# Linear layers as two 64-column matmuls side by side, the last step's two pairs transposed by TensorE, and the experts' pieces laid out anew in an attention and expert kernel

## The chip, the cores and the metric

The kernel runs on one core of a Trainium2 chip, in one launch. The metric is the device time in microseconds (us) of that core; lower is better. Times of a kernel are the median of several runs. The profile, with a trace behind it, belongs to one further execution.

## The reference, cut to what matters

For each of 8 batches of 512 tokens with 256 features, the input is normalised; then attention with 16 heads of 64 features (rotary positions on q and k, a bias that falls with the distance) and a layer of 16 experts, of which each token takes one, both read the normalised input, and the sum of input and both is the output.

```python
qkv = (x @ qkv_w.T).reshape(Bb, Ss, 3, H, D)
...
scores = jnp.einsum('bhqd,bhkd->bhqk', q, k) * SCALE
...
kb = -p * jnp.log1p(a * dist)
attn = jax.nn.softmax(scores + kb[None], axis=-1)
out = jnp.einsum('bhqk,bhkd->bhqd', attn, v)
...
return out @ out_w.T
...
h = jax.nn.relu(jnp.einsum('ecm,emf->ecf', dispatched, w1))
expert_out = jnp.einsum('ecf,efm->ecm', h, w2)
gathered = expert_out[idx, jnp.minimum(loc, C - 1)]
...
x = x + _L0_attn_ref(xn, ...) + _L0_ffn_ref(xn, ...)
```

`x` is 8 x 512 x 256, each expert has w1 of 256 x 1024 and w2 of 1024 x 256 and room for 256 tokens. All is float32.

## The kernel before, in words

**Steps, pairs, units, duos.** The heads go in 4 groups of 4, and a *step* is one group of one batch: 32 steps, s = 0 to 31. A step has two *pairs* of heads (pair 0 and 1), a pair has four blocks of 128 queries (qc 0 to 3). A *unit* is one pair and one block, two units make a *duo*; so a step has four duos (dd = 0 to 3), and the main loop (L850) runs over 128 duos d. The schedule is by hand (L51): each engine's order is that of the program text.

**What a duo does.** In the order of the text: project q or k of a pair of the next step (`project_qk`, L564: two matmuls of 128 x 128 weights and 512 moving columns, and a copy and a rotation on ACT, DVE and POOL); the scores of the two units of the following duo (`score`, L610: for each head a matmul with 64 rows and 512 columns, with bias and minimum on DVE, and the exponential on ACT, which goes to the tile z); in odd duos from the fifth on `attend` (L708: 8 matmuls of 64 columns, one head to each half of the output's partitions) for the pair that was scored a good two duos earlier; `project_out` of step s - 2 in dd 0 (L746); `turn` of the duo's own two units (L640, 32 x 32 transposes in place on DVE); `attended` (L720, normalising the output on DVE); `project_v` in dd 0 and 1 (L587). After a pair's last turn `move` (L646) carries z into pt, transposed by blocks, with 16 DMAs, one for the reciprocals' way through DRAM (rd) and two to bring them back (rb). All of these 19 are issued by SyncE (SP), as are the weights, normalised inputs and the y tiles. `later` (L867) holds DMAs that SP issues in the next duo.

**The experts.** The routing is computed in small parts from duo 16 on (`route`, L311). When it is done the weights of expert 0 are loaded and `begin` is set; from there `expert_work` (L543) yields one *piece* at a time, 8 for each expert: four `expert_hidden` (L507, each 4 products of 256 columns and a relu on ACT) and four `expert_out` (L523, each 4 such products). A duo does 1, 1, 4, and 2 or 3 pieces in dd 0 to 3 (L933). The next expert's input is gathered by POOL after the second piece (`fetch`), transposed by TensorE in the piece with quarter 2 (L554, `expert_in`, L495), and the next weights are put into `later` after the fourth and the eighth piece. The w1 and w2 tiles have two buffers each, one expert's two halves. From duo 108 (`late`, L803) on POOL gathers the experts' output back (`gather`, L759), ACT weighs it and POOL adds it to y.

**PSUM pools.** `ps_sc` has four tiles (scores), `ps_mm` two (q and k, v, output, experts), `ps_av` one, `ps_po` one (experts' output, logits) (L65 to L68).

**The last step.** Pair 1 of step 31 is not turned and moved but goes through `turn_last` (L673): DVE divides z by its sums into zn, TensorE transposes four 128 x 128 blocks of each head into a `ps_mm` tile, and ACT copies them to a tile of its own, which comes from z's three-buffer pool. `attend_last` (L693) is the product with v for it. Pair 0 goes the usual way, by `move`. After the loop (L974 to L983) come attend of (31, 0), attend_last of (31, 1) in two halves and the last output. In duo 127 the text has `attended` of (30, 1) and `project_out` of step 30 ahead of its turn_last (L885 to L886).

Of the kernel before, what the change touches and what calls it, by code (L numbers as in the profile page):

```python
# [33 lines left out]
def attention_and_experts(  # L34
# [472 lines left out]
    def expert_hidden(e, f2):  # L507
        if f2 == 0:
            held["hT", e] = ffn["a"].tile([P, F // P, CAP], F32, tag="hT", name=f"hT_{e}")
        hT, xdT = held["hT", e], held["xdT", e]  # L510
        ph = ps_mm.tile([P, 2, CAP], F32, tag="mm", name=f"ph_{e}_{f2}")
        for i in range(2):
            fc = 2 * f2 + i
            for mc in range(2):
                nc.tensor.matmul(  # L515
                    ph[:, i, :],
                    held["w1", e, fc // 4][:, mc, (fc % 4) * P : (fc % 4 + 1) * P],
                    xdT[:, mc, :],
                    start=(mc == 0), stop=(mc == 1),
                )  # L520
        nc.scalar.activation(hT[:, 2 * f2 : 2 * f2 + 2, :], ph, AF.Relu)

    def expert_out(e, quarter):  # L523
        c, half = divmod(quarter, 2)
        hT = held["hT", e]
        if quarter == 0:
            held["po", e] = ps_po.tile([P, 2, DM], F32, tag="po", name=f"po_{e}")
        po = held["po", e]
        for fc in range(half * 4, half * 4 + 4):
            nc.tensor.matmul(  # L530
                po[:, c, :], hT[:, fc, c * P : (c + 1) * P], held["w2", e, fc // 4][:, fc % 4, :],
                start=(fc == 0), stop=(fc == F // P - 1),
            )
        if quarter == 3:
            ot = ffn["a"].tile([P, 2, DM], F32, tag="eo", name=f"eot_{e}")
            nc.scalar.copy(ot, po)  # L536
            later.append(
                lambda: nc.sync.dma_start(
                    eo[e * CAP : (e + 1) * CAP, :].rearrange("(c p) m -> p c m", p=P), ot
                )  # L540
            )

    def expert_work():  # L543
# [20 lines left out]
    def project_qk(s, pair, part, turn_too=True):  # L564
        g, b = divmod(s, B)
        wq, _ = weights[g]
        ps = ps_mm.tile([P, S], F32, tag="mm", name=f"qk_{s}_{pair}_{part}")
        c0 = part * GC + pair * P
        for mc in range(2):
            nc.tensor.matmul(  # L570
                ps, wq[:, mc, c0 : c0 + P], xnTs[s][:, mc, :], start=(mc == 0), stop=(mc == 1),
            )
# [14 lines left out]
    def project_v(s, i2):  # L587
# [6 lines left out]
        for i in range(2):  # L594
            c0 = (2 * i2 + i) * P
            for mc in range(2):
                nc.tensor.matmul(  # L597
                    ps[:, i, :], xnTs[s][:, mc, c0 : c0 + P], wq[:, mc, 2 * GC :],
                    start=(mc == 0), stop=(mc == 1),
                )  # L600
# [71 lines left out]

    def turn_last(s, pair, qc):  # L673

        if qc == 0:
            pts[s, pair] = zpool.tile([P, 2, TB, S], F32, tag="z", name=f"pt_{s}_{pair}")
        rs = small.tile([P, 2], F32, tag="rs", name=f"rs_{s}_{pair}_{qc}")
        nc.vector.reciprocal(rs, sums[s, pair][:, :, qc])
        for j in range(2):
            zn = rope.tile([P, S], F32, tag="sh", name=f"zn_{s}_{pair}_{qc}_{j}", bufs=3)  # L680
            nc.vector.tensor_scalar(
                zn.rearrange("p (c g k) -> p g c k", g=TB, k=32),
                zts[s, pair][:, j, :, :, qc, :], rs[:, j : j + 1], None, ALU.mult,
            )
            ps = ps_mm.tile([P, TB, P], F32, tag="mm", name=f"zt_{s}_{pair}_{qc}_{j}")
            for kc in range(TB):
                nc.tensor.transpose(ps[:, kc, :], zn[:, kc * P : (kc + 1) * P], ident)
            nc.scalar.copy(pts[s, pair][:, j, :, qc * P : (qc + 1) * P], ps)

    oTs: dict = {}  # L690
    avs: dict = {}

    def attend_last(s, pair, i2):  # L693

        if i2 == 0:
            avs[s, pair] = ps_av.tile([P, S], F32, tag="av", name=f"av_{s}_{pair}")
            oTs[pair] = qkpool.tile([P, S], F32, tag=f"o{pair}", name=f"o_{s}_{pair}", bufs=1)
        av, c = avs[s, pair], slice(i2 * 2 * P, (i2 + 1) * 2 * P)
        for kc in range(TB):
            for j in range(2):  # L700
                c0 = pair * P + j * D
                nc.tensor.matmul(
                    av[j * D : (j + 1) * D, c], vals[s][:, kc, c0 : c0 + D],
                    pts[s, pair][:, j, kc, c], start=(kc == 0), stop=(kc == TB - 1),
                )
        nc.vector.tensor_copy(oTs[pair][:, c], av[:, c])

# [38 lines left out]
    def project_out(s, i2):  # L746
        _, wot = weights[s // B]
        ps = ps_mm.tile([P, 2, DM], F32, tag="mm", name=f"po_{s}_{i2}")
        for i in range(2):
            c0 = (2 * i2 + i) * P  # L750
            for pair in range(2):
                nc.tensor.matmul(  # L752
                    ps[:, i, :], oTs[pair][:, c0 : c0 + P], wot[:, pair, :],
                    start=(pair == 0), stop=(pair == 1),
                )
# [91 lines left out]
    turned_at = {3: 2, 6: 3, 8: 4, 10: 5, 12: 6, 14: 7}  # L847
    routing = route()
    working = begin = None
    for d in range(duos):  # L850
# [8 lines left out]
        if d + 1 < duos:  # L859
            score(*units[2 * d + 2])  # L860
            score(*units[2 * d + 3])
        was = divmod((d - 5) // 2, 2) if half and d >= 5 else None
        if was:
            attend(*was)

# [10 lines left out]
            stores.pop(0)()  # L876


        if dd == 0 and s > 1:
            project_out(s - 2, 0)  # L880
        if d == duos - 1:
            attended(*was)
            project_out(s - 1, 0)
            project_out(s - 1, 1)
            store_y(s - 1, True)  # L885
        (turn_last if final else turn)(*units[2 * d])  # L886
        if was and d < duos - 1:
            attended(*was)
        if d == 1:
            turn_logits(0)  # L890
# [1 line left out]
            turn_logits(1)  # L892
        if d - 1 in turned_at:
            turn_logits(turned_at[d - 1])
        if dd in (0, 1):
# [6 lines left out]
        if dd == 0 and s > 1:  # L902
            project_out(s - 2, 1)
            later.append(lambda s=s: store_y(s - 2, s - 2 >= steps - B + 2))

# [127 lines left out]
```

## Time and profile before

| what | before |
|---|---|
| median of 3 runs | 1273.08 us (1268.95 to 1273.43) |
| the profiled execution's own time | 1280.13 us |
| its span in the trace | 1278.4 us |
| busy: TensorE, DVE, ACT, POOL | 1219.7, 893.5, 611.7, 617.4 us |
| weight loads of TensorE | 670.1 us |
| DMA, SP's queue | 177104 packets, 240.98 MB, 73.6% of 16 engines |
| TensorE's clock, mean of the span | 0.988 of full |

Busy times of different engines overlap. Line numbers such as L570 are lines of the kernel before. In a group's name, `out<-in`, come the tiles by the names of the program: qk, v, sc, av, po and ph are the PSUM tiles of the products. The trace records two matmuls for each float32 product of the text, and one for each transpose; so a `project_qk` shows as 4, a `score` duo as 8, an `attend` as 16. A matmul's end is modelled, so the distance of the starts of two of them says more than a length. "SPq" is SP issuing.

### The profile page before, as it was taken

The page shows a single profiled execution, that of the slowest core. Times are in us where ns is not written, and L with a number is a line of the kernel's source. Part 1 is how long each engine was busy: PE and PEld are TensorE (multiplying, and loading weights), DVE is VectorE, ACT ScalarE, POOL GpSimd, SP SyncE. Part 2 cuts the span into 40 slices and gives each one's busy share as a digit, 9 for nine tenths or more (in the row PEclk, how much of TensorE's full clock was granted, in tenths as well). Part 3 has the DMA queues.
Part 4 walks back from the last instruction along what each step waited for, and adds up shares of the span by engine and source line. Part 5 has one row for each costly group of instructions (what it writes and reads, how often), then busy time and mean ns, then how long its engine had stood idle before and what let it go on. Part 6 is the DMA issues. An engine that isn't in the chain of part 4 may idle for free.

```text
span 1278.4 us, 17383 instructions
## 1 busy us (share of the span) xinstructions
PE 1219.7 (95%) x5070; PEld 670.1 (52%) x5070; DVE 893.5 (70%) x2265; ACT 611.7 (48%) x1425; POOL 617.4 (48%) x614
## 2 busy tenths in 40 slices
PE   8799999999999999999999999999999999999867
PEld 5344444444455565655556565555656554444434
DVE  7998897999866556566556566655665568878762
ACT  6566653466443343445533444443446435555551
POOL 5766654455543343334433344433435334686840
PEclk9899998999999999999999999999999999999989
DMA  4589998888788898878786887877768768999985
GB/s 133 144 209 245 263 229 211 199 199 207 198 221 211 235 238 234 210 198 212 205 217 166 240 203 213 222 209 193 188 195 214 198 156 200 209 227 228 214 229 143
DMA packets 184670, 264.15 MB, mean 207 GB/s; under 512 B 32176, under 2 KB 96448, under 8 KB 184576
## 3 DMA queue, kind: packets, MB, share of 16 engines
q1 hardware_dynamic: 177104, 240.98, 73.6%
q0 software_dynamic: 6368, 20.99, 6.0%
q10 hardware_dynamic: 1104, 1.07, 0.2%
q8 instruction: 41, 0.67, 0.2%
q14 instruction: 53, 0.43, 0.1%
HBM read 99.39 MB, written 31.44 MB: 102 GB/s over the span
## 4 chain that ended last, share of the span: by engine, by line
PE 71%; DMA 13%; DVE 6%; SPq 5%; ACT 3%; issue 1%; POOL 1%; ACTq 0%; DVEq 0%
PE sc L620 13%; PE qk L570 13%; PE av L713 12%; PE po L752 8%; PE v L597 8%; PE ph L515 8%; PE po L530 7%; DMA xnT<-xnd 5%; SPq L658 4%; DMA pt<-z 4%; DMA w<-in_w 3%; DVE z L631 2%; DVE z L644 1%; ACT z L635 1%; ACT xn L245 1%
## 5 line engine op out<-in xcount | busy, mean ns | idle before, releaser
L583 POOL TENSOR_TENSOR t<-t,cos_t 128x512 f32<-128x512 f32 (+1 forms) x126 | 161.3, 1280 | 556.0 <-ACT t L579 555.8
L635 ACT ACTIVATE z<-z,st 128x512 f32<-128x512 f32 x512 | 363.3, 711 | 44.8 <-DVE st L631 36.4
L631 DVE CUSTOM_DVE_ANT_1 z<-sc,kb 128x512 f32<-128x512 f32 x512 | 322.6, 686 | 35.3 <-PE sc L620 26.5
L644 DVE STREAM_TRANSPOSE z<-z 128x512 f32<-128x512 f32 x504 | 319.8, 682 | 0.0
L570 PE MATMUL qk<-xnT,wq 128*128 128x512 f32 x512 | 247.8, 607 | 12.6 <-DMA xnT<-xnd 8.1
L620 PE MATMUL sc<-t,t 64*128 64x512 f32 x1024 | 255.3, 617 | 0.7 <-DVE t L585 0.7
L713 PE MATMUL av<-pt,v 128*64 128x512 f32 x1008 | 235.5, 610 | 9.1 <-DMA pt<-z 8.3
L579 ACT COPY t<-qk 128x512 f32<-128x512 f32 x125 | 73.2, 585 | 341.8 <-DVE sh L574 341.8
L574 DVE LOAD_MASK_SELECT sh<-qk x128 | 1.8, 14 | 241.4 <-PE qk L570 239.4
L620 PEld LDWEIGHTS sc<-t,t 64*128 64x128 f32 x1024 | 88.5, 186 | 155.0 <-issue 127.7
L585 POOL TENSOR_TENSOR t<-t,sh 128x512 f32<-128x512 f32 (+1 forms) x126 | 160.5, 1274 | 9.9
L584 POOL TENSOR_TENSOR sh<-sh,sin_t 128x512 f32<-128x512 f32 (+1 forms) x126 | 161.0, 1278 | 0.0
L713 PEld LDWEIGHTS av<-pt,v 128*64 128x64 f32 x1008 | 69.2, 139 | 167.0 <-issue 136.6
L570 PEld LDWEIGHTS qk<-xnT,wq 128*128 128x128 f32 x512 | 94.4, 192 | 101.5 <-issue 69.0
L752 PE MATMUL po<-wo,o 128*128 128x256 f32 x512 | 124.3, 386 | 0.2 <-DVE o L723 0.2
L597 PE MATMUL v<-wq,xnT 128*128 128x256 f32 x512 | 124.1, 385 | 0.0
L530 PE MATMUL po<-w,hT 128*128 128x256 f32 x512 | 120.5, 383 | 3.5 <-DMA w<-in_w 2.5
L515 PE MATMUL ph<-xdT,w 128*128 128x256 f32 x512 | 118.8, 382 | 2.2 <-ACT eot L536 1.4
L752 PEld LDWEIGHTS po<-wo,o 128*128 128x128 f32 x512 | 94.5, 190 | 36.4 <-issue 11.1
L597 PEld LDWEIGHTS v<-wq,xnT 128*128 128x128 f32 x512 | 94.7, 190 | 35.8 <-DVE z L644 14.6
L515 PEld LDWEIGHTS ph<-xdT,w 128*128 128x128 f32 x512 | 95.6, 190 | 27.7 <-ACT z L635 4.9
L530 PEld LDWEIGHTS po<-w,hT 128*128 128x128 f32 x512 | 95.0, 190 | 28.7 <-issue 9.4
(147 smaller groups left out, 828.3 us busy)
## 6 DMA issues: line engine op xcount, KB each, us to landing
pt<-z SPq DMA_DIRECT2D x1008, 128.0 KB, 3.2
w<-in_w SPq DMA_DIRECT2D x64, 512.0 KB, 7.4
rb<-rd SPq DMA_DIRECT2D x126, 128.0 KB, 4.1
xnT<-xnd SPq DMA_DIRECT2D x28, 512.0 KB, 5.9
yd<-y SPq DMA_DIRECT2D x26, 512.0 KB, 5.2
y<-yd SPq DMA_DIRECT2D x24, 512.0 KB, 6.8
xrd<-xn POOLq DMA_DIRECT2D x8, 512.0 KB, 6.8
xnd<-xnT POOLq DMA_DIRECT2D x8, 512.0 KB, 7.8
```

Source lines behind the costliest of these rows:

```text
L515: nc.tensor.matmul(ph[:, i, :], held["w1", e, fc // 4][:, mc, (fc % 4) * P : (fc % 4 + 1) * P], xdT[:, mc, :], start=(mc == 0), stop=(mc = ...
L530: nc.tensor.matmul(po[:, c, :], hT[:, fc, c * P : (c + 1) * P], held["w2", e, fc // 4][:, fc % 4, :], start=(fc == 0), stop=(fc == F // P ...
L570: nc.tensor.matmul(ps, wq[:, mc, c0 : c0 + P], xnTs[s][:, mc, :], start=(mc == 0), stop=(mc == 1),)
L583: eng.tensor_tensor(t[:, c], ps[:, c], cos_t[:, c], ALU.mult)
L584: eng.tensor_tensor(sh[:, c], sh[:, c], sin_t[:, c], ALU.mult)
L597: nc.tensor.matmul(ps[:, i, :], xnTs[s][:, mc, c0 : c0 + P], wq[:, mc, 2 * GC :], start=(mc == 0), stop=(mc == 1),)
L620: nc.tensor.matmul(sc[j].rearrange("p (g c k) -> p g c k", g=TB, k=32), q[r, qc * P : (qc + 1) * P], k[r, :].rearrange("p (c g k) -> p g c ...
L631: nc.vector.tensor_tensor_reduce(z, sc[j].rearrange("p (g c k) -> p g c k", g=TB, k=32), bias, -0.125, 3.0e38, ALU.add, ALU.min, st[:, j : ...
L635: nc.scalar.activation(z, z, AF.Exp, bias=st[:, j : j + 1], scale=-1.0, accum_out=sums[s, pair][:, j, qc : qc + 1],)
L644: nc.vector.transpose(z, z)
L713: nc.tensor.matmul(av[j * D : (j + 1) * D, :].rearrange("p (a q) -> p a q", q=P), vals[s][:, kc, c0 : c0 + D], pts[s, pair][:, j, :, kc, : ...
L752: nc.tensor.matmul(ps[:, i, :], oTs[pair][:, c0 : c0 + P], wot[:, pair, :], start=(pair == 0), stop=(pair == 1),)
```

## The change

There are three parts.

1. A new function `product` splits a product by its 128 output rows into two matmuls of 64 weight columns each, one to each half of the output's partitions. It takes the place of the single matmul in `project_qk`, `project_v`, `project_out`, `expert_hidden` and `expert_out`.
2. The experts' transposes: quarter 0 of an expert puts the next one on a list `coming`, and the next duo's text calls `expert_in` right behind its scores. The fixed numbers of pieces (1, 1, 4, 2 or 3) are replaced by shares 1, 1, 4, 2 of a total that ends with the duo before `late`, at most 4 in a duo.
3. In the last step both pairs go through `turn_last`, in the duo after their own (units 2d - 2 and 2d - 1), except that the last duo does four. Its copies go back into z, so it needs no tile of its own, and the second head's transposes use `ps_po`. `attend` of (30, 1) comes in duo 126 (before: 127); both halves of v of the last step are projected in duo 124, ahead of the output of step 29; `move` is not called in step 31. After the loop: attend_last of (31, 0) in one part, project_out of step 30 and its store, attend_last of (31, 1) in two, project_out of step 31.

```diff
+    def product(o, w, v, start, stop):
+
+        for c in range(2):
+            half = slice(c * D, (c + 1) * D)
+            nc.tensor.matmul(o[half], w[:, half], v, start=start, stop=stop)
...
-                if quarter == 2 and e + 1 < E:
-                    expert_in(e + 1)
+                if quarter == 0 and e + 1 < E:
+                    coming.append(e + 1)
...
-        if qc == 0:
-            pts[s, pair] = zpool.tile([P, 2, TB, S], F32, tag="z", name=f"pt_{s}_{pair}")
...
-            ps = ps_mm.tile([P, TB, P], F32, tag="mm", name=f"zt_{s}_{pair}_{qc}_{j}")
+            pool, tag = (ps_po, "po") if j else (ps_mm, "mm")
+            ps = pool.tile([P, TB, TB, 32], F32, tag=tag, name=f"zt_{s}_{pair}_{qc}_{j}")
             for kc in range(TB):
-                nc.tensor.transpose(ps[:, kc, :], zn[:, kc * P : (kc + 1) * P], ident)
-            nc.scalar.copy(pts[s, pair][:, j, :, qc * P : (qc + 1) * P], ps)
+                nc.tensor.transpose(
+                    ps[:, kc].rearrange("p c k -> p (c k)"), zn[:, kc * P : (kc + 1) * P], ident
+                )
+            nc.scalar.copy(z, ps)
...
-    def attend_last(s, pair, i2):
+    def attend_last(s, pair, i2, n):
...
-        final = (s, pair) == units[-1][:2]
+        final = s == steps - 1
...
+        while coming:
+            expert_in(coming.pop())
         was = divmod((d - 5) // 2, 2) if half and d >= 5 else None
+        if d >= duos - 2:
+            was = (s - 1, 1) if dd == 2 else None
...
-        if d == duos - 1:
-            attended(*was)
-            project_out(s - 1, 0)
-            project_out(s - 1, 1)
-            store_y(s - 1, True)
-        (turn_last if final else turn)(*units[2 * d])
-        if was and d < duos - 1:
+        if final and dd == 0:
+            project_v(s, 0)
+        if final:
+            if dd > 0:
+                turn_last(*units[2 * d - 2])
+        else:
+            turn(*units[2 * d])
+        if was:
             attended(*was)
...
-        (turn_last if final else turn)(*units[2 * d + 1])
+        if final and dd == 0:
+            project_v(s, 1)
+        if final:
+            if dd > 0:
+                turn_last(*units[2 * d - 1])
+            if dd == TB - 1:
+                turn_last(*units[2 * d])
+                turn_last(*units[2 * d + 1])
+        else:
+            turn(*units[2 * d + 1])
...
-            for _ in range((1, 1, 4, 2 + s % 2)[dd]):
+            share = (1, 1, 4, 2)
+            due = 8 * E * sum(share[k % TB] for k in range(begin + 1, d + 1)) / sum(
+                share[k % TB] for k in range(begin + 1, late))
+            for _ in range(min(4, math.ceil(due - 1e-6) - pieces)):
+                pieces += 1
...
-    attend(s, 0)
-    attended(s, 0)
-    for i2 in range(2):
-        attend_last(s, 1, i2)
+    outs = dict(oTs)
+    attend_last(s, 0, 0, TB)
+    lasts = dict(oTs)
+    oTs.update(outs)
     for i2 in range(2):
-        project_out(s, i2)
+        project_out(s - 1, i2)
+    store_y(s - 1, True)
+    oTs.update(lasts)
+    for i2 in range(2):
+        attend_last(s, 1, i2, 2)
```

In the five functions named in part 1 the call `nc.tensor.matmul(` becomes `product(` and nothing else; `attend_last` reads z in place of pt and takes its output tiles from `ps_sc` or `ps_av` and from tiles of the experts that are free by then.

More of the change, by code (lines that the diff above doesn't have):

```diff
@@ L514, in expert_hidden @@
             for mc in range(2):
-                nc.tensor.matmul(
+                product(
                     ph[:, i, :],
@@ L529, in expert_out @@
         for fc in range(half * 4, half * 4 + 4):
-            nc.tensor.matmul(
+            product(
                 po[:, c, :], hT[:, fc, c * P : (c + 1) * P], held["w2", e, fc // 4][:, fc % 4, :],
@@ L541, in expert_out @@
             )
+    coming: list = []
     def expert_work():
@@ L569, in project_qk @@
         for mc in range(2):
-            nc.tensor.matmul(
+            product(
                 ps, wq[:, mc, c0 : c0 + P], xnTs[s][:, mc, :], start=(mc == 0), stop=(mc == 1),
@@ L596, in project_v @@
             for mc in range(2):
-                nc.tensor.matmul(
+                product(
                     ps[:, i, :], xnTs[s][:, mc, c0 : c0 + P], wq[:, mc, 2 * GC :],
@@ L679, in turn_last @@
         for j in range(2):
+            z = zts[s, pair][:, j, :, :, qc, :]
             zn = rope.tile([P, S], F32, tag="sh", name=f"zn_{s}_{pair}_{qc}_{j}", bufs=3)
             nc.vector.tensor_scalar(
-                zn.rearrange("p (c g k) -> p g c k", g=TB, k=32),
-                zts[s, pair][:, j, :, :, qc, :], rs[:, j : j + 1], None, ALU.mult,
-            )
-            ps = ps_mm.tile([P, TB, P], F32, tag="mm", name=f"zt_{s}_{pair}_{qc}_{j}")
+                zn.rearrange("p (c g k) -> p g c k", g=TB, k=32), z, rs[:, j : j + 1], None,
+                ALU.mult,
+            )
+            pool, tag = (ps_po, "po") if j else (ps_mm, "mm")
+            ps = pool.tile([P, TB, TB, 32], F32, tag=tag, name=f"zt_{s}_{pair}_{qc}_{j}")
             for kc in range(TB):
-                nc.tensor.transpose(ps[:, kc, :], zn[:, kc * P : (kc + 1) * P], ident)
-            nc.scalar.copy(pts[s, pair][:, j, :, qc * P : (qc + 1) * P], ps)
+                nc.tensor.transpose(
+                    ps[:, kc].rearrange("p c k -> p (c k)"), zn[:, kc * P : (kc + 1) * P], ident
+                )
+            nc.scalar.copy(z, ps)
     oTs: dict = {}
     avs: dict = {}
-    def attend_last(s, pair, i2):
+    def attend_last(s, pair, i2, n):
         if i2 == 0:
-            avs[s, pair] = ps_av.tile([P, S], F32, tag="av", name=f"av_{s}_{pair}")
-            oTs[pair] = qkpool.tile([P, S], F32, tag=f"o{pair}", name=f"o_{s}_{pair}", bufs=1)
-        av, c = avs[s, pair], slice(i2 * 2 * P, (i2 + 1) * 2 * P)
+            pool, tag = ((ps_sc, "sc"), (ps_av, "av"))[pair]
+            avs[s, pair] = pool.tile([P, S], F32, tag=tag, name=f"av_{s}_{pair}")
+            oTs[pair] = ffn["a"].tile([P, S], F32, tag=("xe", "eo")[pair], name=f"o_{s}_{pair}")
+        av, c = avs[s, pair], slice(i2 * n * P, (i2 + 1) * n * P)
         for kc in range(TB):
@@ L702, in attend_last @@
                 nc.tensor.matmul(
-                    av[j * D : (j + 1) * D, c], vals[s][:, kc, c0 : c0 + D],
-                    pts[s, pair][:, j, kc, c], start=(kc == 0), stop=(kc == TB - 1),
+                    av[j * D : (j + 1) * D, c].rearrange("p (q c k) -> p q c k", c=TB, k=32),
+                    vals[s][:, kc, c0 : c0 + D],
+                    zts[s, pair][:, j, kc, :, i2 * n : (i2 + 1) * n, :].rearrange(
+                        "p c q k -> p q c k"),
+                    start=(kc == 0), stop=(kc == TB - 1),
                 )
@@ L751, in project_out @@
             for pair in range(2):
-                nc.tensor.matmul(
+                product(
                     ps[:, i, :], oTs[pair][:, c0 : c0 + P], wot[:, pair, :],
@@ L849, in attention_and_experts @@
     working = begin = None
+    pieces = 0
     for d in range(duos):
@@ L876, in attention_and_experts @@
             stores.pop(0)()
-        if dd == 0 and s > 1:
+        if dd == 0 and s > 1 and not final:
             project_out(s - 2, 0)
-        if d == duos - 1:
-            attended(*was)
-            project_out(s - 1, 0)
-            project_out(s - 1, 1)
-            store_y(s - 1, True)
-        (turn_last if final else turn)(*units[2 * d])
-        if was and d < duos - 1:
+        if final and dd == 0:
[6 more added lines that the diff above has]
+        if was:
             attended(*was)
@@ L894, in attention_and_experts @@
             turn_logits(turned_at[d - 1])
-        if dd in (0, 1):
+        if dd in (0, 1) and not final:
             project_v(s, dd)
-        (turn_last if final else turn)(*units[2 * d + 1])
+        if final and dd == 0:
[8 more added lines that the diff above has]
+            turn(*units[2 * d + 1])
         if dd == 1 and 4 <= s + 2 < steps:
@@ L902, in attention_and_experts @@
         if dd == 0 and s > 1:
+            if final:
+                project_out(s - 2, 0)
             project_out(s - 2, 1)
```

## The prediction

> **What bounds the kernel now.** I read the page first, then busy time by stretch, TensorE's own timeline in a typical stretch, the waits of TensorE, and at last the DMA issues of SyncE (SP) and the chain of waits near the end. The page says that TensorE is the engine to look at, and that 18% of the ending chain is transfers (DMA) and their issue (SPq):
>
> ```profile
> PE 1219.7 (95%) x5070; PEld 670.1 (52%) x5070; DVE 893.5 (70%) x2265; ACT 611.7 (48%) x1425; POOL 617.4 (48%) x614
> ...
> PE 71%; DMA 13%; DVE 6%; SPq 5%; ACT 3%; issue 1%; POOL 1%; ACTq 0%; DVEq 0%
> ```
>
> Busy time by stretch shows that these are different stages. The first line below is the stretch with the experts' products, the second the four steps before the last, the third the last step and the tail:
>
> ```profile
> 361.00:1048.00 687.00, 680.93 (x2808) 409.29 (x2806) 409.99 (x994) 296.64 (x676) 271.94 (x225) 1.00 0.78 208
> 1108.00:1218.50 110.50, 101.27 (x375) 45.71 (x374) 87.43 (x218) 62.45 (x156) 85.86 (x70) 0.97 0.95 227
> 1218.50:1278.40 59.90, 42.54 (x202) 24.07 (x200) 25.49 (x62) 17.46 (x42) 12.79 (x10) 0.91 0.69 178
> ```
>
> In the first, TensorE idles 687.0 - 680.9 = 6.1 us: it is the bound. In the second it idles 9.2 us while the DMA engines are 95% busy; in the last 17.4 us. So I price the middle by TensorE's time, the late steps by the transfers, and the tail by its own chain.
>
> TensorE's timeline in the middle (start us, length us, line, matmuls in the run):
>
> ```profile
> 589.85 3.65 PE L713 MATMUL av<-pt,v 128*64 128x512 f32 x16
> 593.44 1.99 PE L597 MATMUL v<-wq,xnT 128*128 128x256 f32 x8
> 595.27 1.89 PE L515 MATMUL ph<-xdT,w 128*128 128x256 f32 x8
> 596.99 1.88 PE L570 MATMUL qk<-xnT,wq 128*128 128x512 f32 x4
> 598.80 1.99 PE L620 MATMUL sc<-t,t 64*128 64x512 f32 x8
> 600.72 1.99 PE L515 MATMUL ph<-xdT,w 128*128 128x256 f32 x8
> ```
>
> Read the starts. ph to qk is 1.72 us for 8 matmuls: 0.216 us each, no loss. Runs of the 512-wide kind go at 0.429 us per step (qk: 4 steps, 1.716). Where the array's shape changes there is more: qk to sc 1.81 - 1.716 = 0.094 lost in leaving; the sc run 1.92 - 4 x 0.429 = 0.20 (entering 0.10, leaving 0.09 to 0.10); the av run 3.59 - 8 x 0.429 = 0.16, of which the spacing of single matmuls puts 0.05 on entering; v after av 1.83 - 1.73 = 0.10 for entering. The 16 av matmuls, 64 columns each, took 8 steps: two run side by side at the pace of one full product.
>
> **What the Trainium skill says.** "TensorEngine Tiling (Array Packing)", Key Properties: "Changing tiling mode (not just tile) drains the TensorE". The trace agrees: 0.09 us at each change. "TensorE: Matmul & The Clock Gate", LDWEIGHTS, has a weight load take columns / 1.2 ns, 107 for 128 and 53 for 64; the entering loss here is 0.10 for full shapes and 0.05 for the 64-column shape, so it agrees (the loads' own records, 190 and 137 ns, are longer). The same page, Part 1, has the clock halve after an idle window of about 3.4 us; here the av run at 1247.86, behind a 5.9 us wait, took 5.56 us where others took 3.65.
>
> **Part 1, products as two of 64 columns.** They then have av's shape. In two duos now: full, sc, full, sc, av: two full stretches (0.10 + 0.09 each), two sc (0.20 each), av 0.15, together 0.93 to 0.95. Afterwards product stretch and sc twice, av joined to a product stretch: 2 x 0.145 + 2 x 0.20 = 0.69. Gain 0.25 us in two duos. Between duos 41 and 107 (experts) these are 33.5 x 0.25 = **-8.4 us**, on the bound. The pace itself I take as unchanged, also for 256-wide halves, which the tail shows:
>
> ```profile
> 1265.80 1.95 PE L702 MATMUL av<-pt,v 128*64 128x256 f32 x16 [0.79 <-DVE o L723]
> ```
>
> 16 in 8 steps: (1.95 - 0.38 of one) / 7 = 0.22 us, as the full product's 0.216. TensorE's records double for 2560 matmuls; nothing in this row says that this costs. Bounds: 0 to +58 ns per 256-wide step, if two loads of 137 ns had to queue (274 against 216); below nothing is excluded because the streaming is the same. I take 0.
> Before duo 41 some work keeps its full shape and now stands between two changes: 6 transposes of normed batches, 8 of logits, some 6 routing products, at 0.19 us each +3.8 us, against 12.5 x 0.25 + 5.5 x 0.25 = -4.5. This stage also waits for transfers (xnT). I take **0**, ends -3 and +3.
>
> **Part 2, the experts' transposes behind the scores.** Now they stand among full products (four take 0.44 us, no loss). Among column halves they would cost two changes, behind a score one more than there is: 15 x 0.19 = **+2.9 us**. Their inputs come from a POOL gather issued three pieces earlier, with the PSUM copy on DVE behind four score reductions; cover is a duo of 7 us or more.
>
> **Part 3, even spread.** Now 8.5 pieces per step, done in duo 101; then up to duo 107, 7.6 per step, the same number. Laying both sequences out by duo, a weight load (7.4 us to landing) is issued in the very duo that needs it for 6 of 15 experts now, for 3 afterwards. Of the 6.1 us of idle the waits of TensorE name the weights for 3.3 and ACT at the same places for 2.4; half gone: **-3 us** (ends -6 and +2). A new wait: the last expert's store enters SP's queue behind 16 moves in duo 108 and lands about 18 us into it; the first gather back, on POOL in duo 108, ran at 8.5 us. Behind it on POOL stand the rotations of duo 109 to 111, behind its landing the weighing on ACT (some 8 us late), and behind that exponentials for duo 112. The rotations have two duos of slack and SP is late by then anyway: I take 0, ends 0 and +4.
> Sum at the start of duo 108: -8.4 + 2.9 - 3.0 + 0 = **-8.5 us**.
>
> **Late steps.** SP issues 38 transfers per step at some 0.6 us; without expert products it falls behind. DVE finished turning pair (30, 1) at 1220.82, and SP came to it at 1228.03:
>
> ```profile
> 1220.61 0.21 DVE L653 STREAM_TRANSPOSE turned<-inverse 128x32 f32<-128x32 f32 x1
> ```
> ```profile
> 1225.11 1.65 SPq L666 DMA_DIRECT2D rb<-rd  x2
> 1226.81 0.62 SPq L736 DMA_DIRECT2D y<-yd  x1
> 1227.53 0.39 SPq L794 DMA_DIRECT2D out<-early  x1
> 1228.03 3.36 SPq L658 DMA_DIRECT2D pt<-z  x4
> 1232.16 0.53 SPq L663 DMA_DIRECT2D rd<-turned  x1
> 1232.74 10.58 SPq L658 DMA_DIRECT2D pt<-z  x12
> ```
>
> So from about duo 109 on TensorE's gain buys nothing, and SP's pace holds. What counts is when SP enters this stage: now 2.5 us behind (1109.28 against 1106.74), because step 26 had no experts; afterwards 26 has them, and SP should start at once, as at 1024. Shift of SP: -8.5 - 0.3 (duos 108, 109) - 2.3 = **-11.1 us** (ends -5 and -17).
>
> **Tail.** Today the ACT copy of the first turned pair waits for a buffer until the last move of (30, 1) lands (1245.32), and attend(30, 1) starts at 1247.86. Then it needs only the landing: 1245.3 - 11.1 = 1234.2; TensorE, there about 1226, waits and runs at half clock. From there: attend 5.56; six turn_last left in TensorE's order, where one 0.95 and each further 1.31 (start to start of the two zt runs at 1258.97 and 1260.28), plus 0.25 for DVE behind attended, 7.8; attend_last(31, 0) 3.6; project_out(30) 3.5; attend_last(31, 1) 3.5; project_out(31) 3.5. New forms: the copy back into z in runs of 32, taken as the ACT copy of today (0.59 us; at worst the exponential's 0.71, which writes z so: +1.5 in six units), and attend_last reading runs of 32, as the scores do at full pace. Together 27.5, and 4.7 us as now from TensorE's end to the span's: 1266.4. Removing the moves of (31, 0), 19 issues, saves nothing more: they stand behind the path. The tail by itself, from attend(30, 1), is 32.2 against 30.5 now.
> Span 1278.4 to 1266.4, **-12.0 us**. The profiled execution took 1280.13 us, 7 us above the median of the runs, 1273.08; I take the difference over unscaled: **1261 us**. About 0.5%, 6.4 us, is what a measurement of this kernel can tell from no change.
>
> **Rivals.**
> A, 13%: SP's lag was only the backlog of step 26, and the late steps follow TensorE. For it: SP keeps up elsewhere. Against: 38 x 0.6 plus waits is over the 29 us of a step. attend(30, 1) then comes 8 us earlier, at full clock (-1.9): 1251 us.
> B, 18%: the gain is given back late: weight waits stay (+3), SP starts as late as now (+2.3), the gather's wait costs 3: -3.7, 1269 us, no measurable change.
> C, 7%, slower: the halves don't run side by side where both read the same moving rows (av's read different ones). Place: 2560 product steps in the middle. From 12 / 2560 = 4.7 ns per step it eats all; at its bound, loads in turn, 58 ns x 2048 = 119 us, 1380 us. Against: the L702 row, at full pace.
> The likeliest, 62%, has 1255 to 1267.
>
> **How the numbers follow.** The likeliest time is 1261. 1249 to 1270 takes in A, B and the ends of the unknown terms, and leaves out C. Faster by over 0.5% is the likeliest, A and a bit of B: 0.79; within 0.5% the rest of B: 0.14; slower C: 0.07.
>
> **What would show it.** Product runs start 0.216 and 0.429 us per step apart, without loss between av and products; the stretch 361 to 1048 shrinks by some 8 us; SP's first move of step 27 starts with its turning; attend(30, 1) waits for transfers; six zt runs about 1.3 us apart. I am wrong if product steps grow, if the late steps shorten, or if ACT stalls at the weighing in duo 110.

## The result, and the profile after

| what | before | after | after / before, 95% interval |
|---|---|---|---|
| median, 20 runs of each | 1273.12 us | 1268.07 us | 0.9965 [0.9951, 0.9979] |
| once more, in the last group of runs | 1273.81 us (33 runs) | 1269.38 us (22 runs) | 0.9961 [0.9944, 0.9978] |
| the profiled execution, span | 1278.4 us | 1265.8 us | |

The change saves about 5 us, 0.35 to 0.4%; the prediction had 12. The span that it worked out, 1266.4 us, came within 0.6 us of the one measured. That is the puzzle of this case. Further profiles of the kernel before explain a part of it, and the close end itself turns out to be luck.

From the page of the changed kernel, busy times and the shares of the ending chain:

```profile
PE 1213.3 (96%) x7662; PEld 558.0 (44%) x7662; DVE 894.0 (71%) x2267; ACT 615.4 (49%) x1433; POOL 617.9 (49%) x614
...
PE 70%; DMA 12%; SPq 8%; DVE 5%; ACT 2%; issue 2%; POOL 1%; DVEq 0%; ACTq 0%
```

TensorE is 6.4 us less busy, although its records rose from 5070 to 7662. Busy time by stretch (bounds, length, then PE, PEld, DVE, ACT, POOL, TensorE's clock, DMA share, GB/s): the middle, the late steps, the last step with the tail:

```profile
361.00:1048.00 687.00, 682.32 (x4548) 330.45 (x4550) 425.85 (x1038) 305.51 (x700) 283.63 (x234) 1.00 0.80 213
1100.00:1203.70 103.70, 97.46 (x528) 38.06 (x524) 86.40 (x218) 61.82 (x156) 90.77 (x74) 1.00 0.95 235
1203.70:1265.80 62.10, 47.30 (x298) 24.46 (x296) 27.57 (x65) 21.95 (x52) 14.47 (x11) 0.95 0.52 136
```

The middle still has 4.7 us of idle, the late steps still have the DMA engines at 95%, and the tail is longer than before (62.1 against 59.9 us) with less DMA (52% against 69%). TensorE's timeline in the middle:

```profile
587.60 1.90 PE L196 MATMUL v<-wq,xnT 128*64 128x256 f32 x16
589.33 1.90 PE L196 MATMUL po<-w,hT 128*64 128x256 f32 x16
591.06 1.89 PE L196 MATMUL qk<-xnT,wq 128*64 128x512 f32 x8
592.87 1.99 PE L628 MATMUL sc<-t,t 64*128 64x512 f32 x8
```

Sixteen halves of v take 1.73 us from start to start, 8 steps of 0.216, as the eight full products did, and nothing is lost between v, po and qk. The halves run side by side, and rival C is out.

DVE's turning of pair (30, 1), and from the timeline of SP what it issued next:

```profile
1205.80 0.21 DVE L661 STREAM_TRANSPOSE turned<-inverse 128x32 f32<-128x32 f32 x1
```
```profile
1211.45 1.38 SPq L674 DMA_DIRECT2D rb<-rd  x2
1212.88 0.64 SPq L751 DMA_DIRECT2D y<-yd  x1
1213.62 0.40 SPq L809 DMA_DIRECT2D out<-early  x1
1214.12 4.56 SPq L666 DMA_DIRECT2D pt<-z  x4
```

SP comes to this pair 8.1 us after it was turned (7.2 before). At step 27 it was on time in the changed kernel (its lag, the time from a pair's turning to its first move, was -0.1 us), as worked out. So SP gets late again within two steps, but it enters this stage sooner. The attend of this pair still waits for its transfers:

```profile
1230.62 6.50 PE L728 MATMUL av<-pt,v 128*64 128x512 f32 x16 [3.49 <-DMA pt<-z]
```

### The profile page after: what moved, and what is told of

The parts are those of the page before. It is cut to its first block, busy times and chain, and to the rows that moved or that the text cites. A ratio compares the mean times of both kernels' runs of the same rounds, so it can differ in the third digit from the quotient of the medians.

```text
span 1265.8 us, 22538 instructions
## 1 busy us (share of the span) xinstructions
PE 1213.3 (96%) x7662; PEld 558.0 (44%) x7662; DVE 894.0 (71%) x2267; ACT 615.4 (49%) x1433; POOL 617.9 (49%) x614
## 4 chain that ended last, share of the span: by engine, by line
PE 70%; DMA 12%; SPq 8%; DVE 5%; ACT 2%; issue 2%; POOL 1%; DVEq 0%; ACTq 0%
PE po L196 16%; PE sc L628 13%; PE qk L196 13%; PE av L728 12%; PE ph L196 8%; SPq L666 7%; PE v L196 6%; DMA pt<-z 5%; DMA xnT<-xnd 2%; DVE z L639 2%; DMA rd<-turned 1%; DMA w<-in_w 1%; ACT xn L251 1%; SPq L674 1%; DVE z L652 1%
## 5 line engine op out<-in xcount | busy, mean ns | idle before, releaser
L639 DVE CUSTOM_DVE_ANT_1 z<-sc,kb 128x512 f32<-128x512 f32 x512 | 322.6, 686 | 32.2 <-PE sc L628 24.4
L196 PE MATMUL qk<-xnT,wq 128*64 128x512 f32 x1024 | 246.6, 603 | 12.6 <-DMA xnT<-xnd 8.6
L196 PEld LDWEIGHTS qk<-xnT,wq 128*64 128x64 f32 x1024 | 71.5, 138 | 118.5 <-issue 84.7
L196 PE MATMUL po<-wo,o 128*64 128x256 f32 x1024 | 122.6, 382 | 0.3 <-issue 0.3
L196 PE MATMUL v<-wq,xnT 128*64 128x256 f32 x1024 | 121.5, 380 | 0.0
L196 PE MATMUL po<-w,hT 128*64 128x256 f32 x1024 | 118.3, 380 | 1.5 <-DMA w<-in_w 1.5
L196 PE MATMUL ph<-xdT,w 128*64 128x256 f32 x1024 | 117.6, 380 | 0.4 <-DVE inverse L659 0.4
L643 ACT ACTIVATION_READ_ACCUMULATOR z<-z,st 128x1 f32 x512 | 95.8, 187 | 0.0
L196 PEld LDWEIGHTS v<-wq,xnT 128*64 128x64 f32 x1024 | 72.9, 137 | 50.1 <-issue 9.4
L582 DVE STREAM_SHUFFLE sh<-qk 128x512 f32<-128x512 f32 x128 | 93.7, 732 | 0.7
L196 PEld LDWEIGHTS po<-wo,o 128*64 128x64 f32 x1024 | 70.8, 137 | 52.9 <-issue 9.8
```

Source lines behind the costliest of these rows:

```text
L196: nc.tensor.matmul(o[half], w[:, half], v, start=start, stop=stop)
L639: nc.vector.tensor_tensor_reduce(z, sc[j].rearrange("p (g c k) -> p g c k", g=TB, k=32), bias, -0.125, 3.0e38, ALU.add, ALU.min, st[:, j : ...
L643: nc.scalar.activation(z, z, AF.Exp, bias=st[:, j : j + 1], scale=-1.0, accum_out=sums[s, pair][:, j, qc : qc + 1],)
```

## The experiments

Before is the unchanged kernel in the same group of runs. "Scores of duo n" is the start of that duo's first score in a trace; long waits are gaps of TensorE over 0.25 us beyond a run's own pace between the scores of duos 44 and 108, and switching losses the shorter ones where its shape changes.

**The kernel before, repeated**, with no edit.

> The kernel before, unchanged, profiled once more. Theory 1 (the profiled execution of before was some 7 us slow in its late steps, and the prediction took its saving from that): the span is near 1271 us, the scores of duo 108 start near 1082 as in the first profile, and from there to the end it is about 189 us instead of 196. Rival (the middle is what varies): duo 108 comes near 1075 and the rest is again 196 us. If the span is again near 1278, both fall.

> A second repeat of the kernel before, to see how much a stage varies by itself. Theory 1: duo 108 again within 2 us of 1082, and what varies lies behind it, with the number of microseconds by which SyncE is late for pair (30, 1). Rival: duo 108 varies by 5 us or more.

They took 1274.62 and 1273.59 us, spans 1272.8 and 1271.9. The execution that the prediction was made from, 1280.13, lies at the slow edge: of the 249 timed runs of before in all groups, six took as long or longer. Side by side:

| us | the first profile of before | before_a, before_b | after, after_c | predicted move | measured, mean of two to mean of two |
|---|---|---|---|---|---|
| scores of duo 44 | 385.5 | 387.3, 385.2 | 384.2, 387.3 | 0 | -0.5 |
| scores of duo 108 | 1082.5 | 1080.6, 1079.5 | 1074.0, 1077.9 | -8.5 | -4.1 |
| start of attend(30, 1) | 1247.9 | 1242.0, 1241.0 | 1230.6, 1234.7 | -13.7 | -8.9 |
| end | 1278.4 | 1272.8, 1271.9 | 1265.8, 1268.4 | -12.0 | -5.3 |
| switching losses, duos 44 to 108 | 30.2 | 30.3, 30.4 | 24.7, 24.8 | -5.5 | -5.6 |
| long waits, there | 7.0 | 3.4, 4.4 | 7.2, 7.9 | -3.0 | +3.7 |

The last column of the row "end" agrees with the timed -5. Each entry of that column is from two executions to two, so single waits in it are uncertain by microseconds (see below). The waits of TensorE from 361 to 1048 us (engine, line, what it waited for: total, times, longest) in the first profile of before, in before_a, in the changed kernel and, for the weights (`w`) alone, in *tail* (below), whose middle is that of before:

```profile
PE po L530 <- DMA w<-in_w: 2.5, 3, 1.3
PE ph L515 <- ACT eot L536: 1.4, 2, 0.7
PE po L530 <- ACT hT L521: 1.0, 1, 1.0
PE ph L515 <- DMA w<-in_w: 0.8, 2, 0.5
```
```profile
PE po L530 <- ACT hT L521: 1.0, 1, 1.0
PE ph L515 <- issue: 0.7, 1, 0.7
PE ph L515 <- ACT eot L536: 0.7, 1, 0.7
PE po L530 <- DMA w<-in_w: 0.4, 1, 0.4
```
```profile
PE xdp L506 <- DMA rd<-turned: 2.2, 1, 2.2
PE po L196 <- DMA w<-in_w: 1.5, 2, 0.9
PE xdp L506 <- DMA xg<-xrd,sidx: 0.6, 1, 0.6
```
```profile
PE ph L515 <- DMA w<-in_w: 1.9, 1, 1.9
PE po L530 <- DMA w<-in_w: 1.4, 2, 1.0
```

In the first fence the weights hold TensorE for 3.3 us, in the second for 0.4, in the fourth, with the same instructions there, for 3.3 again; before_b has 1.2. So the waits that the spread was to halve change from execution to execution, and the first profile had them at their highest. The third shows a new one: the pace of the shares lets four pieces of expert 0 fall into one duo, so expert 1's input (L506) is wanted at 386.9 and its gather, issued at 379.2 to 380.5, lands at 389.4.

**One part at a time.** *products*: only the new function, in its five places.

```diff
-                nc.tensor.matmul(
+                product(
```

> Only the products as two of 64 columns; the experts' transposes stay among them. 33.5 x 0.25 = 8.4 us saved between duos 41 and 107, less 15 transposes at two changes each (0.33 us) = 5, so duo 108 comes about 3.4 us earlier. Theory 1: the end moves by the same 3 us, since SyncE enters its late stage earlier by as much: ratio 0.997 to 0.998. Rival (transfers set the late steps' end by themselves): no change, ratio 1.000. Rival C (halves not side by side): slower by 1% or more.

1274.46 against 1274.66 us, ratio 1.0005 [0.9988, 1.0022]: nothing. Its switching losses are some 27 us; the transposes, left among column halves, cost some of the gain.

*spread*: only the shares.

```diff
-            for _ in range((1, 1, 4, 2 + s % 2)[dd]):
+            for _ in range(min(4, math.ceil(due - 1e-6) - pieces)):
+                pieces += 1
```

> Only the even spread of the experts' pieces; products whole, the experts' transposes at quarter 2, the last step as before. Theory 1: fewer weight waits between duos 44 and 108 (some 5 us in the repeats of before, now about half: -2.5) and SyncE enters step 27 without being late (-2): ratio 0.996 to 0.998. Rival (the pieces' places don't matter because the late steps take as long as their transfers): 1.000.

1269.6 against 1274.49 us, 0.9956 [0.994, 0.9973]: as much as the whole change. Long waits in the middle are 6.0 us here and 3.6 in a second profile of the same kernel (spread_c, below), within the range of before; the stretch from duo 108 to 125 lasts 129.6 and 130.9 us, where the profiles of before have 136.0, 133.7 and 133.0. The spread pays late, where SP is on time at step 27 (lag 0.1 us).

*tail*: only the third part.

```diff
-        final = (s, pair) == units[-1][:2]
+        final = s == steps - 1
...
+            if dd > 0:
+                turn_last(*units[2 * d - 2])
```

> Only the last step's part: both pairs by TensorE transposes. SyncE's work up to pair (30, 1) is the same, so attend(30, 1) starts at most 2.5 us earlier, and the chain from there takes 35 us (as in the kernel after) where the kernel before has 30.5: theory 1 says +2 us, ratio 1.001 to 1.002. Rival (the tail is where the change gains, since SyncE has 19 transfers less): 3 us or more faster, ratio 0.997 or less.

1274.99 against 1274.66 us, 1.0016 [0.9999, 1.0033]: no gain, and a loss of 2 us if anything.

*prod_spread*: parts 1 and 2 together, without the third.

> The kernel after without the last step's part. Theory 1: all that the change gains lies ahead of the last step, and the last step gives back 2 to 3 us (62.1 us from duo 125 to the end against 58.6 to 59.9): so this one is 2 us faster than the kernel after, ratio 0.994 to 0.995 to before. Rival (the tail gains): slower than the kernel after, 0.998 or more.

1269.52 against 1274.49 us, 0.9957 [0.9942, 0.9973]: the same as the spread alone, in the same group of runs.

**Where does the products' gain stay?** *mid_products* is prod_spread with split products in duos 41 to 107 only; *mid_c* is the same kernel once more beside *spread_c*, the spread alone; *early_products* has the spread and splits only in duos 0 to 40.

```diff
+        if not split:
+            nc.tensor.matmul(o, w, v, start=start, stop=stop)
+            return
...
+        split[:] = [1] * (40 < d < late)
```

> The even spread and the experts' transposes behind the scores, with split products between duos 41 and 107 only, and the last step as before. Where products stood alone, TensorE's saving in the middle (-4 us between duos 44 and 108) was there in the trace and the end did not move; the first 44 duos were 1 to 3 us longer with them. Theory 1 (the loss of the first duos takes it): ratio 0.992 to 0.993, some 4 us better than the spread alone. Rival (what TensorE saves is lost again in the late steps, whatever the first ones do): 0.9955 as the spread alone.

> Before with the even spread alone, as the measure for the two kernels beside it. Both theories: 0.996 of before, as it measured earlier (0.9956); its stretch from the scores of duo 44 to those of duo 108 lasts 694 us, and that from duo 108 to duo 125 lasts 130 us.

> The even spread, and products as two of 64 columns in duos 0 to 40 only. Theory 1, the early duos give back what the middle gains: slower than the spread alone by 1.5 to 4 us (ratio to before 0.997 to 0.999), with the stretches up to duo 44 together at 365 us or more, where kernels without split products have 362 to 364.5. Theory 2, the early duos are neutral and later waits take up the middle's gain: as the spread alone, 0.996, and 363 us.

> The even spread, and products as two of 64 columns in duos 41 to 107 only, with the experts' transposes behind the scores. Theory 1: faster than the spread alone by the middle's 4 to 6 us, ratio to before 0.991 to 0.993; duo 44 to 108 in 688 us. Theory 2: as the spread alone, 0.996, although the middle takes 688 us, and then the stretch from duo 108 to the end is longer than the spread's by as much.

mid_products 0.995 [0.9935, 0.9966] (1267.4 us); then, in one group, spread_c 0.996 [0.9945, 0.9976] (1267.99), early_products 0.997 [0.9956, 0.9984] (1269.19), mid_c 0.9961 [0.9943, 0.9978] (1266.64). The early duos, from the scores of duo 0 to those of duo 44, last 362.2 us with split products and 363.4 without, so this pair shows no give-back as large as theory 1 wants. It doesn't rule out a small one: early_products was 1.2 us slower than spread_c at the median, and over all profiles that keep the work of these duos they last 364.7 us in eight with split products there and 363.1 in ten without, with a scatter of 359.9 to 368.8. The middle of mid_c took 688.8 us and of spread_c 692.0, but what follows was shorter, not longer (187.0 against 191.4; 191.9 in mid_products, the same kernel), so theory 2 is not borne out either. The profile of mid_c is of the fastest of its 14 runs, 1259.57 us. Over all kernels here that keep the work of these duos, the middle is 689.4 us in nine profiles with split products and 694.0 in nine without; but the first nine executions lay on average 1.3 us below their kernels' medians and the other nine 2.3 above. So a part of these 4.6 us may be chance, and the timed comparisons, each with an interval of some 2 us to either side, leave 0 to 2 us for the products. The losses fall as worked out; why so little of it shows in the time is open.

**The waits in the middle.** *after_fetch* gathers the next expert's input one piece earlier. *best1* is prod_spread with the same edit.

```diff
-                if f2 == 1 and e + 1 < E:
+                if f2 == 0 and e + 1 < E:
                     fetch(e + 1)
```

> The kernel after with the next expert's input gathered one piece earlier. In the trace of after the second expert's gather was issued 7.6 us before its transposes and TensorE lost 3.1 us waiting and 1.6 at half clock. If this wait is where the saved weight waits went, it is gone and the ratio falls from 0.9965 to 0.993; the long waits between duos 44 and 108 fall from 7.2 to some 2.5 us. Rival (SyncE's lateness there absorbs it): no change against after, 0.9965.

> Products and spread with the earlier gather, last step as before: the sum of the two runs above, ratio 0.990 to 0.992 if theory 1 holds in both points; 0.9965 or more if neither.

0.9981 [0.9962, 1.0] and 0.9956 [0.9938, 0.9975]. The wait at L506 is gone in after_fetch; four waits for the experts' weights, of 1.0 to 1.7 us, end at 522, 567, 612 and 656 us (after_c has three there, 3.4 us in all). No gain from this edit shows.

*one_per_step* is before with one expert to each step: 1, 1, 4, 2 pieces from duo 44 on and none earlier.

```diff
+            for _ in range((1, 1, 4, 2)[dd] if d >= late - 4 * E else 0):
```

> The kernel before with exactly one expert to each step from duo 44 on, 1, 1, 4, 2 pieces in dd 0 to 3, so that it ends in duo 107 as the even spread does, but every weight load has at least a duo's time in all 16 experts. If weight waits are what is left of the middle, long waits between duos 44 and 108 fall from 5 or 6 us to 2 or less and the ratio is 0.992 to 0.994; the late steps as with the even spread (129 to 130 us from duo 108 to 125). Rival (the lighter late steps are all of the spread's gain): 0.9955 as the spread.

0.9992 [0.9975, 1.001]. From 390 to 1048 us the waits of TensorE sum to 0.3 us, none for weights: their loads then stand well ahead of their use. But two waits for transfers of a pair and of the normalised input, 3.7 and 3.6 us, end at 382 and 389 us, just where the experts' work begins; why was not followed up. In the time nothing is gained.

*best2* joins one_per_step, split products in the middle, the transposes behind the scores and the earlier gather, with the old last step.

> One expert to a step, split products between duos 41 and 107 only, transposes behind the scores with the earlier gather, the last step as before. If both theories above hold their gains add: 0.989 to 0.990. If neither, 0.9955.

1266.81 us (7 runs), 0.9941 [0.9917, 0.9965]: the lowest ratio among the kernels without part 3, though its interval overlaps that of the change.

**What sets the late steps' pace: SP's issuing or the DMA engines?** *spread_act* is the spread with a quarter of the moves from step 27 on issued by ACT.

```diff
-                nc.sync.dma_start(
+                (nc.scalar if s >= 27 and qi == 3 else nc.sync).dma_start(
```

> The even spread, and in steps 27 to 30 a quarter of the moves' DMAs (4 of 16) issued by ACT in place of SyncE; the same bytes. If SyncE's issue time sets the late steps' pace (as the prediction has it), its 16 issues fall to 12, some 2.5 us in each of 8 pairs, its lateness for pair (30, 1) falls below 5 us and the end comes 3 to 5 us earlier than with the spread alone: 0.992 to 0.993. Rival (the transfers themselves set it: DMA engines at 95%): no gain, 0.9955 or slower.

1298.38 us, 1.0191 [1.016, 1.0223]. This did not tell them apart, as ACT itself stood in the way. From its timeline:

```profile
1185.89 2.94 ACTq L658 DMA_DIRECT2D pt<-z  x4
1188.93 0.59 ACT L579 COPY t<-qk 128x512 f32<-128x512 f32 x1 [2.51 <-DMA pt<-z]
```

Four issues hold ACT for 2.9 us, with the next q and k and the exponentials behind them.

*spread_halves* issues each late move as two of half the size: the same bytes, 32 issues more per step.

```diff
+                for j in range(2) if s >= 27 else ():
+                    nc.sync.dma_start(
+                        pt[g * 32 : (g + 1) * 32, j, qi].rearrange("p c q -> p (c q)"),
+                        z[qi * 32 : (qi + 1) * 32, j, g].rearrange("p c q k -> p (c q k)"),
+                    )
```

> The even spread, with each of the sixteen transfers of a move from step 27 on issued as two of half the size: the same bytes and rows, 64 issues more in a step. Theory S, what SP spends on issuing sets the late steps' pace, some 0.6 us for each whatever its size: about 20 us more in each step, duo 108 to 125 in 190 us or more, and some 60 to 80 us more in all. Theory D, the DMA engines' work sets it and SP only waits for room: no change, within 3 us of the spread alone. In between: an issue costs less when it is smaller, and the time grows by the part that does not shrink.

1351.15 us, 1.0609 [1.0584, 1.0634], 79 us more than before and 83 more than spread_c. (The 64 in the expectation is a wrong count.) The stretch from duo 108 to 125 took 186.2 us, against 130.9 in spread_c. SP's timeline, and the late steps by stretch in this kernel and in spread_c:

```profile
1241.62 15.06 SPq L659 DMA_DIRECT2D pt<-z  x24
1256.73 1.30 SPq L673 DMA_DIRECT2D rb<-rd  x2
```
```profile
1108.00:1270.00 162.00, 118.17 (x388) 57.71 (x387) 90.66 (x228) 63.63 (x162) 96.32 (x79) 0.84 0.57 153
```
```profile
1108.00:1215.00 107.00, 101.12 (x390) 47.64 (x389) 90.50 (x228) 64.07 (x163) 91.44 (x74) 1.00 0.94 229
```

An issue of half the size still takes 15.06 / 24 = 0.63 us, and SP needs 51.9 us for a step (the mean of steps 28 to 30, from first move to first move) where spread_c needs 34.0: 17.9 / 32 = 0.56 us for each issue added, nearly its whole price, while the DMA engines fall from 94% busy to 57%. Had the DMA engines set the pace, SP would have had room for a good part of the added issues. So an issue on SP is on the path here, and the prediction's reading of these steps holds.

**The tail.** In the changed kernel one scaling of z on DVE took 2.58 us beside an add on POOL. *after_c* is the changed kernel again; *after_add* lets DVE add the last batch's experts after the last turn_last.

```diff
-            if k == 3:
+            if k == 3 and bb < B - 1:
                 combine(bb, ys[steps - B + bb])
...
+    nc.vector.tensor_tensor(ys[s], ys[s], held.pop(("gt", B - 1)), ALU.add)
     attend_last(s, 0, 0, TB)
```

> The changed kernel once more, as the measure for the kernel beside it, and a second profile of it. If its first profile is an ordinary execution: ratio to before 0.996 to 0.998, span within 1262 to 1270 us, scores of duo 108 from 1071 to 1078 us, and 34 to 36 us from the start of attend(30, 1) to the end. One scaling of z in the last step takes over 2 us beside POOL's last add of the experts' output.

> The changed kernel with the experts' output of the last batch added by DVE after the last turn_last, where DVE idles for 5 us, and not by POOL in the middle of them. Theory L, that add on POOL holds up DVE's scaling of z and this is the term by which the tail was mis-sized: no scaling over 0.5 us after attend(30, 1), the tail from attend(30, 1) on shorter by about 2.1 us (33 where it is 35), and the time as much lower, 0.998 of the unchanged. Rival, the slow scaling is covered by the copies of ACT or by TensorE at half clock: the tail stays at 35 us.

after_c 0.9961 [0.9944, 0.9978], after_add 0.994 [0.992, 0.996] (1267.01 us), 2.4 us lower at the median; the intervals overlap, so the time alone doesn't settle it. The timeline of all engines of after_c, then that of DVE in after_add:

```profile
1240.88 0.88 DVE L689 TENSOR_SCALAR zn<-z,rs 128x512 f32<-128x512 f32 x2
...
1241.95 2.98 DVE L689 TENSOR_SCALAR zn<-z,rs 128x512 f32<-128x512 f32 x2
1242.23 2.40 POOL L797 TENSOR_TENSOR y<-y,room 128x1024 f32<-128x1024 f32 x1 [17.07 <-DMA y<-yd]
```
```profile
1242.36 0.88 DVE L689 TENSOR_SCALAR zn<-z,rs 128x512 f32<-128x512 f32 x2
...
1243.42 0.88 DVE L689 TENSOR_SCALAR zn<-z,rs 128x512 f32<-128x512 f32 x2
...
1247.67 1.22 DVE L1011 TENSOR_TENSOR y<-y,room 128x1024 f32<-128x1024 f32 x1
```

Two scalings take 0.88 us, but 2.98 where POOL's add begins during the first of them. Without that add it is 8.0 us from the first transpose behind attend(30, 1) to attend_last(31, 0), where after has 10.1 and after_c 9.8, and attend(30, 1) to the end lasts 31.9 us (1236.2 to 1268.1), where after has 35.2 and after_c 33.6. The prediction had 32.2: theory L holds in the trace. By their ratios after_add and best2 are the lowest of all here; what they change lies in different places, and the two together were not tried.

## Why the prediction was wrong

The direction was right, and TensorE's losses fell as worked out; the size was not right: -5 us for -12. By its own steps:

- *"The profiled execution took 1280.13 us, 7 us above the median of the runs, 1273.08; I take the difference over unscaled."* This is the step that failed first. That execution lay at the slow edge, and what made it longer than the two repeats (2.6 to 3.6 us more of long waits in the middle, then 2.3 to 3.0 us more from duo 108 to 125) lay in just the stages that the change was priced in. 12.6 us separate the two first profiles, only 5.3 the means of two executions of each. That the worked-out end, 1266.4, was met is luck: on the mean of after and after_c duo 108 came 2.0 us later than worked out, from there to attend(30, 1) it took 3.5 us less, and the tail 2.3 us more.
- *"half gone: -3 us"*, the weights' waits: they did not fall. From 376 to 1080 us TensorE waited for weights 3.3, 0.4, 1.2, 1.7 and 3.3 us in the five profiles with the old pieces per duo (before, its repeats, products, tail), and 1.1 to 5.0 in the eleven with the even spread and the gather in its old place, on the mean 2.0 and 2.8. The +3.7 of the table sets two executions beside two; over these sixteen profiles the long waits are about 5 us in both. So the term is about 0 in place of -3, which is most of the miss of 4.4 at duo 108. Its 6.1 us of idle came from one execution. The runs one_per_step and best2, with no wait for weights after 390 us, show what it takes to remove such waits, loads that lie well ahead and not an even pace; in one_per_step, where nothing else changes, it brought nothing.
- *"their cover is a duo of 7 us or more"* failed at one expert: the spread puts the gather for expert 1 and its use 7.6 us apart. This made 2.8 us of waits in after, and the attend behind them took 5.33 us where others take 3.65.
- *Part 1, -8.4, and part 2, +2.9*: right as losses, -5.5 worked out and -5.6 measured; the pace is unchanged. In the time of a kernel it is worth 0 to 2 us, for a reason that stays open; the early duos, taken at 0, may take back some 1.5 us. Rival C is out; its 2560 steps are those of the whole kernel and not of the middle alone.
- *"Shift of SP"*: right. Lag at step 27 is -0.1 us in after, 1.8 and 2.4 in the repeats, so -2.2 against -2.3 predicted. Between duo 108 and attend(30, 1) the move is -4.8 for -5.2. Rival A is out, since that attend still waits for its transfers (3.49 us in after). ACT did stall at the weighing, for 3.9 us in after, which the prediction named as a sign of being wrong; TensorE worked through it without a wait, so the 0 taken for it was right.
- *The tail, "32.2 against 30.5 now"*: 35.2 and 33.6 measured, against 30.8 and 30.9 in the repeats. The steps of transposes were counted nearly right (8.0 us in after_add for 7.8). What was not counted is the add on POOL, named in no step, which the new order of the last step brings beside them: 1.8 to 2.1 us. In after the attend ahead of them was also longer, 6.5 us for 5.56.
- *Rival B* had the size (1269 us), in part by luck: the waits stay, as it said, and something is given back late. Its place was wrong. SP did start sooner, and the give-back is in the tail.

By parts, timed: spread -4.9 and -3.7 us (predicted -3 and, at SP's start, -2.3, so nearly right in sum and wrong in place), products 0 to -2 (predicted -5.5), last step 0 to +2 (predicted +1.7 less 2.5 for the copy's wait that it removes).

## What to carry to other kernels

Before pricing anything by a profile, set its own time beside the runs. Where it lies at their edge, and where a term is a few small waits, take a second and a third profile first: here the same waits for weights came to 0.4 us in one execution and 3.3 in another. An even pace by itself did not remove such waits; loads laid well ahead of their use did. And when a step is moved in time, ask for each engine in it what the neighbouring engines now do at that moment, not only what is queued on the engine itself: here an add on POOL held up a scaling on DVE.

## What was not expected of the hardware

A scaling on DVE (128x512, float32, SBUF to SBUF) that starts while POOL adds two tiles is not slowed in proportion, it behaves as if it waited until the add is over. Free it took 0.47 to 0.49 us; in eight cases, in five profiles with the new last step, it took 0.82, 1.56, 1.72, 2.22, 2.31, 2.58, 2.58 and 2.66 us, and ended always 0.28 to 0.31 us after the add. Where it had clearly started first, by 0.05 us or more, it was not lengthened (0.49 us with 0.44 overlapping). The Trainium skill has this in "SBUF — State Buffer", section "SBUF: two separate sides": the port pair of the two engines "is an **exclusive lock**, not a bandwidth split", and whichever starts first keeps it for its whole instruction. The page says this of a DVE operation that uses both of its port pairs; no record here tells whether this scaling does. The numbers agree with a lock, and after_add puts the price on the path at about 2 us.

An issue of a transfer on SP took 0.6 us at 64 KB as at 128 KB.
